# A feed-forward stage whose transposes move from TensorE to VectorE's 32 by 32 squares and an exchange through DRAM

## The chip, the cores and the metric

One core of a Trainium2 chip runs the whole program. The metric is the device time of one execution in microseconds (us), the median of several runs. The engines are named as in the profile: PE (TensorE, with PEld for its weight loads), DVE (VectorE), ACT (ScalarE), POOL (GpSimd) and SP, whose queue issues nearly all DMAs. They run side by side and wait for each other through semaphores. SBUF is the on-chip memory of 128 partitions, PSUM the memory into which PE writes.

## What is computed

Three blocks, each added to x (16 x 64 rows of 512): a cross-attention from x to a context of 16 x 512 rows, a differential self-attention, and a feed-forward block. The change is in the last one alone:

```python
def fp4_quant_dequant(x):                  # blocks of 16 along the last dim
    scale = maximum(max(abs(xb)) / 6.0, 1e-12)
    q = _GRID[searchsorted(_MID, abs(xb / scale))] * sign(xb) * scale
def fp4_linear(x, w):
    return einsum('bsk,nk->bsn', fp4_quant_dequant(x), fp4_quant_dequant(w))
...
xn = layernorm(x)                          # 1024 rows of 512
gate, y = fp4_linear(xn, w_gate), fp4_linear(xn, w_up)      # 1408 columns
h = silu(gate) * y
x = x + fp4_linear(h, w_down)              # back to 512 columns
```

## The kernel before, in words

**Tiles.** The 1024 rows of x are eight row tiles t = 0 to 7 of 128 rows. The 1408 hidden columns are three chunks c = 0, 1, 2 of 512, 512 and 384. A step of the feed-forward stage is one pair (t, c); there are 24, in the order (0,0), (0,1), (1,0), (1,1), (0,2), (1,2), and then (2,0), (2,1), (2,2), (3,0) and so on to (7,2). Steps 0 to 2 are written out by hand among the last pieces of the self-attention (`SelfAttention.rest`, L1623 to L1652). `FeedForward.rest` does the others.

**A step.** `gate` (L1736) and `up` (L1746) multiply the normalised, quantised and transposed x tile by two weight chunks. Each product is three terms: every operand is held as a high and a low half (x as `fx`), and PE adds high x high, high x low, low x high, 12 matmuls for 512 rows of contraction. Both results lie in one PSUM pair `gu`, of which there are two. `gated` (L1753) is ACT's Silu (L1759) and DVE's product (L1760), giving h. `fp4_steps` (L180) quantises h, in order: DVE's block maximum (L194), two small scalings (L195, L196), a reciprocal (L197), the scaling of h by it (L199), the exponent mask (L202), ACT's L205, DVE's L207 and L208, and the scaling back (L210). For h all are on DVE apart from L205; for x, L199 and L210 are on GpSimd. `turn_h` (L1767) transposes h in 128 x 128 squares on PE (`ht`, L171), and `split` (L127) makes the high half `hh` on ACT (L129) and the low half `hl` on DVE (L130). `down` (L1785) multiplies these by w_down and collects `dn` in PSUM over the three chunks of a tile: 12 matmuls, or 9 for chunk 2, of which the last third reads `hl`. After chunk 2 DVE adds x (L1812, `y`) and SP stores the tile.

**The x tiles.** `norm_steps` (L1707) cuts the norm and quantisation of tile t into seven pieces: the moments (DVE, then three small operations on GpSimd, L148 to L160), the shift (ACT, L166), and the five parts of `fp4_steps`. `turn` (L1722) transposes the result on PE (`xt`) and splits it into `fx`.

**Order.** `step(n)` of L1835 names the work of a round: gate of step n, `turn_h` of step n-2, up and `hidden` of n, perhaps a norm, `down` of step n-3, perhaps `turn` of the next x tile. `Common.in_order` (L82) ties every instruction given so far to the one before it on its engine. It is called once, at the end of `SelfAttention.rest` (L1652), so up to there each engine keeps the order of the program (`FeedForward.rest` comes after the call); a scheduler places what comes later, and may put it ahead, between instructions that are tied to each other. Buffers come from pools by tag; a tag with `bufs=1` is one buffer, whose next user waits for the last reader of the one before.

**The chip's own squares.** While the weights are quantised (`Quantise.piece`, L277), DVE transposes each 32 x 32 square of a tile in place of the whole (`nc.vector.transpose`, L287); the weights were rearranged beforehand so that this is enough.

Of the kernel before, what the change touches and what calls it, by code (L numbers as in the profile page):

```python
# [9 lines left out]
F32 = mybir.dt.float32  # L10
F32R = mybir.dt.float32r
# [3 lines left out]
ALU = mybir.AluOpType  # L15
# [4 lines left out]
P = 128  # L20
D = 512
KC = D // P
# [4 lines left out]
NT = B * S // P  # L27
# [18 lines left out]
def f32(t):  # L46

    return t.bitcast(F32)


class Common:
# [125 lines left out]
        for _ in self.fp4_steps(*args, **kwargs):  # L177
            pass

    def fp4_steps(self, pool, w, n, name, first=None, second=None, tag="q_e"):  # L180
        nc = self.nc
        first, second = ((nc.vector, nc.gpsimd)[bool(by)] for by in (first, second))
        nb = n // BLK

        def blocks(t):
            return t.rearrange("p (n b) -> p n b", b=BLK)

        def spread(t):
            return t.unsqueeze(2).to_broadcast([P, nb, BLK])

        m = self.small.tile([P, nb], F32, tag="q_m", name=f"qm_{name}")
        s = self.small.tile([P, nb], F32, tag="q_s", name=f"qs_{name}")
        e = pool.tile([P, n], F32, tag=tag, name=f"qe_{name}")
        nc.vector.tensor_reduce(m, blocks(w), AX.X, ALU.max, apply_absolute_value=True)  # L194
        nc.vector.tensor_scalar(s, m, 1.0 / 6.0, 1e-12, ALU.mult, ALU.max)  # L195
        nc.vector.tensor_scalar(m, s, 1.0 + SHADE, None, ALU.mult)  # L196
        nc.vector.reciprocal(m, m)  # L197
        yield True
        first.tensor_tensor(blocks(w), blocks(w), spread(m), ALU.mult)  # L199
        yield True  # L200

        nc.vector.tensor_scalar(  # L202
            e.bitcast(U32), w.bitcast(U32), 0x7F800000, None, ALU.bitwise_and
        )
        nc.scalar.activation(e, e, AF.Relu, bias=self.mmagic, scale=MAGIC)  # L205
        yield True
        nc.vector.scalar_tensor_tensor(w, e, MAGIC, w, ALU.add, ALU.add)  # L207
        nc.vector.scalar_tensor_tensor(w, w, MAGIC, e, ALU.subtract, ALU.subtract)  # L208
        yield True
        second.tensor_tensor(blocks(w), blocks(w), spread(s), ALU.mult)  # L210
        yield True
# [6 lines left out]
class Scratch:  # L218


    def __init__(self, ctx, tc):
        pool = ctx.enter_context(tc.tile_pool(name="scratch", bufs=1, space=DRAM))

        def dram(name, shape):
            return pool.tile(shape, F32, tag=name, name=name)


        self.q = [dram(f"q_d{g}", [P, KC, GT * P]) for g in range(NT // GT)]
        self.k = [dram(f"k_d{g}", [P, KC, GT * P]) for g in range(NT // GT)]
        self.v = [dram(f"v_d{p}", [P, D]) for p in range(NT)]  # L230
        self.rs = [dram(f"rs_d{b}", [1, N]) for b in range(B)]

        self.gu = {
            (w, c): dram(f"{w}_d{c}", [P, 2, KC, n])
            for w in ("g", "u")
            for c, (_, n) in enumerate(CHUNKS)
        }
        self.dn = [dram(f"d_d{c}", [P, 2, n // P, D]) for c, (_, n) in enumerate(CHUNKS)]


class Quantise:
# [1063 lines left out]
class SelfAttention:  # L1305
# [269 lines left out]
    def rest(self, ff, last):  # L1575

        first, second = (ff.norm_steps(t) for t in range(2))  # L1580
        norms = iter(first[:2] + second[:1] + first[2:4] + second[1:2] + first[4:] + second[2:])


        parts = {3: (1, 0, 1), 4: (1, 2, 1), 5: (1, 2, 0), 6: (0, 2, 0), 7: (1, 2, 0)}

        def steps(n, part):
            for _ in range(parts[n][part] if n in parts else 0):
                next(norms)()

        for n in range(2, NT):  # L1590
            self.product(n, "Wq")
            self.cosines(n, "Wq")
            self.scale(n - 2)
            self.sum(n - 1)
            self.product(n, "Wk")
            if n == NT - 1:
                ff.weights(("g", 1))
            self.mix(n - 1)
            self.turn_o(n - 2)
            self.low_o(n - 2)  # L1600
            self.sines(n, "Wq")
            self.add(n, "Wq")
            self.product(n, "Wv")
            if n == NT - 1:
                ff.weights(("u", 1), ("d", 0))
            self.values(n)
            if n + 1 < NT:
                self.norm(n + 1)
            self.cosines(n, "Wk")
            self.sines(n, "Wk")  # L1610
            steps(n, 0)
            self.add(n, "Wk", self.nc.vector)
            if n == NT - 1:
                ff.turn(0)
            self.out(n - 2)
            last.get(n, lambda: None)()
            if n == 2:
                ff.weights(("g", 0), ("u", 0))
            steps(n, 1)
            self.end(n)  # L1620
            steps(n, 2)
        assert not list(norms)
        self.scale(NT - 2)  # L1623
        self.sum(NT - 1)
        ff.gate((0, 0))
        self.mix(NT - 1)
        ff.up((0, 0))
        ff.gated((0, 0))
        self.turn_o(NT - 2)
        self.low_o(NT - 2)  # L1630
        ff.turn(1)
        ff.gate((0, 1))
        self.turn_w(NT - 1)
        ff.quantise((0, 0))
        ff.weights(("d", 1))
        ff.gate((1, 0))
        self.weigh(NT - 1)
        self.squares(NT - 1)
        self.rms(NT - 1)
        self.out(NT - 2)  # L1640
        ff.weights(("g", 2))
        ff.up((0, 1))
        self.scale(NT - 1)
        ff.hidden((0, 1))
        ff.up((1, 0))
        self.turn_o(NT - 1)
        self.low_o(NT - 1)
        ff.hidden((1, 0))
        ff.turn_h((0, 0))
        self.out(NT - 1)  # L1650
        ff.weights(("u", 2), ("d", 2))
        self.cm.in_order()  # L1652


class FeedForward:


    def __init__(self, tc, cm, sc, w1, w2, out):
        self.tc, self.cm, self.nc, self.sc, self.out = tc, cm, tc.nc, sc, out
        self.w1, self.w2 = w1, w2  # L1660
        self.W, self.st = {}, {}

        self.steps = [(t, c) for t in range(2) for c in range(2)] + [(t, 2) for t in range(2)]
        self.steps += [(t, c) for t in range(2, NT) for c in range(len(CHUNKS))]

    def weights(self, *names):

# [39 lines left out]
    def norm_steps(self, t):  # L1707

        cm, w2, st = self.cm, self.w2, self.st

        def begin():
            st["mv", t] = mv = cm.small.tile([P, 3], F32, tag="mv3", name=f"mv_f_{t}")
            cm.shift(cm.x[t], f"f_{t}", mv)

        def norm():
            z = st["z", t] = w2.tile([P, D], F32, tag=("g_o", "b_o")[t % 2], name=f"fz_{t}")
            cm.shifted(z, cm.x[t], st.pop(("mv", t)))
            st["fp4", t] = cm.fp4_steps(w2, z, D, f"x_{t}", True, True, tag="one")

        return [begin, norm] + 5 * [lambda: next(st["fp4", t])]  # L1720

    def turn(self, t):  # L1722
        cm, w2 = self.cm, self.w2
# [43 lines left out]
    def turn_h(self, s):  # L1767
        cm, w2 = self.cm, self.w2
        t, c = s
        n = CHUNKS[c][1]  # L1770
        nk = n // P
        pt = cm.tr(f"ht_{t}_{c}")
        cm.transpose_chunks(pt, self.st.pop(("h", s)), nk)
        hh = w2.tile([P, KC, P], F32R, tag="two_h", bufs=2, name=f"hh_{t}_{c}")[:, :nk, :]
        hl = w2.tile([P, KC, P], F32R, tag="two_l", bufs=2, name=f"hl_{t}_{c}")[:, :nk, :]
        src = pt[:, :n].rearrange("p (k n) -> p k n", n=P)
        if s == self.steps[-1]:
            for k in range(nk):
                cm.nc.scalar.copy(hh[:, k, :], src[:, k, :])
            cm.nc.vector.tensor_tensor(hl, src, f32(hh), ALU.subtract)  # L1780
        else:
            cm.split(hh, hl, src)
        self.st["hT", s] = hh, hl

    def down(self, s):  # L1785
        cm, nc = self.cm, self.nc
# [45 lines left out]
                nc.vector.tensor_tensor(y[h], both[h], self.cm.x[t][:, cols], ALU.add)  # L1832
                nc.sync.dma_start(self.out[t * P : (t + 1) * P, cols], y[h])

    def step(self, n):  # L1835
        s = self.steps[n] if n < len(self.steps) else None
        if s:
            self.gate(s)
        if 0 <= n - 2 < len(self.steps):
            self.turn_h(self.steps[n - 2])  # L1840
        if s:
            self.up(s)
            self.hidden(s)
            if s[1] == 2 and 2 <= s[0] < NT - 2:
                self.norm(s[0] + 2)
            elif s in ((1, 1), (0, 2)):
                self.norm(1 + s[1])
        if 0 <= n - 3:
            self.down(self.steps[n - 3])
        if s and (s == (1, 2) or (s[1] == 1 and 2 <= s[0] < NT - 1)):  # L1850
            self.turn(s[0] + 1)

    def rest(self):
        for n in range(3, len(self.steps) + 3):
            self.step(n)


@with_exitstack
# [96 lines left out]
```

## Time and profile before

| what | us |
|---|---|
| median of 3 runs (lowest, highest) | 880.55 (878.98, 880.85) |
| the profiled execution's own time | 881.33 |
| its span, first to last instruction | 879.5 |
| PE's matmuls busy | 871.7 |
| DVE busy | 687.2 |
| ACT busy | 398.8 |
| POOL busy | 296.2 |
| share of the chain that ended last: PE | 93% |
| stretch 704 to 879.5: PE, DVE, ACT, POOL busy | 171.54, 143.57, 48.69, 15.53 |

The chain of waits goes back from the last instruction, at each step to what released it; PE has 93% of it. The last row is the feed-forward stage without its first pieces. In the text, a time such as "at 694.87" is counted from the start of the span. Lines of the profile name an engine, the line of the program (that of a helper, if a helper gave the instruction), what is written and read, and the shapes.

### The profile page before, as it was taken

What the parts mean: (1) busy time and instruction counts of PE and PEld (TensorE: products, weight loads), DVE (VectorE), ACT (ScalarE), POOL (GpSimd) and SP (SyncE); (2) the same over time, 40 slices, a digit from 0 to 9 for tenths busy, and PEclk for the clock granted to TensorE, in tenths of its full rate; (3) what the DMA queues carried; (4) which work ended last, traced back from release to release, by engine and by line L of the source; (5) the groups of instructions that cost most, each with busy time, mean ns of one, the idle gap of its engine ahead of it and who ended that gap; (6) DMA issues with size and microseconds to landing.
All of it is one profiled execution on the core that took longest, in us unless ns stands there. A gap on an engine that the chain in (4) does not pass through costs nothing.

```text
span 879.5 us, 17521 instructions
## 1 busy us (share of the span) xinstructions
PE 871.7 (99%) x6743; PEld 719.2 (82%) x6743; DVE 687.2 (78%) x1457; ACT 398.8 (45%) x787; POOL 296.2 (34%) x341
## 2 busy tenths in 40 slices
PE   8999999999999999999999999999999999999998
PEld 8988787878787888778878888888888888888887
DVE  7734457789788887787888867688998897888876
ACT  5654454544544535354445455554556233332221
POOL 2334234235353352353433622545543120111100
PEclk9999999999999999999999999999999999999999
DMA  8464554644655455435644362240008330000000
GB/s 277 167 233 169 167 163 142 201 143 141 192 164 160 138 174 168 136 111 178 183 134 149 121 198 64 82 192 1 1 3 320 136 144 13 13 13 13 13 12 25
DMA packets 80379, 111.12 MB, mean 126 GB/s; under 512 B 33176, under 2 KB 39080, under 8 KB 79016
## 3 DMA queue, kind: packets, MB, share of 16 engines
q1 hardware_dynamic: 80136, 109.48, 38.2%
q8 instruction: 53, 0.87, 0.4%
q0 software_dynamic: 160, 0.52, 0.2%
q14 instruction: 30, 0.25, 0.1%
HBM read 84.26 MB, written 25.72 MB: 125 GB/s over the span
## 4 chain that ended last, share of the span: by engine, by line
PE 93%; DVE 3%; DMA 2%; ACT 1%; POOL 1%; issue 1%; SPq 0%; ACTq 0%; DVEq 0%; POOLq 0%
PE pv L121 20%; PE pk L121 19%; PE gu L121 13%; PE dn L121 6%; PE sim L967 4%; PE av L1055 4%; PE Wv L121 3%; PE wo L121 3%; PE po L121 2%; PE Wq L121 2%; PE Wk L121 2%; PE prt L1004 2%; PE lq L121 2%; PE lk L121 2%; PE lv L121 1%; PE ht L171 1%
## 5 line engine op out<-in xcount | busy, mean ns | idle before, releaser
L121 PE MATMUL pv<-xvh,x 128*128 128x512 f32 x512 | 133.0, 394 | 0.0
L121 PE MATMUL pk<-x,xkh 128*128 128x512 f32 x512 | 128.2, 392 | 0.0
L121 PEld LDWEIGHTS pv<-xvh,x 128*128 128x128 f32 x512 | 94.8, 188 | 26.2 <-issue 7.0
L121 PEld LDWEIGHTS pk<-x,xkh 128*128 128x128 f32 x512 | 94.9, 188 | 19.5 <-issue 0.4
L990 ACT ACTIVATE pr<-pr,least 128x576 f32<-128x576 f32 x64 | 49.1, 769 | 59.7 <-DVE least L986 59.7
L941 DVE TENSOR_TENSOR k<-pk,row 128x512 f32<-128x512 f32 x64 | 43.2, 675 | 39.2 <-PE pk L121 39.0
L368 POOL TENSOR_TENSOR x<-raw,x 128x512 fp32r<-128x512 f32 x32 | 41.6, 1301 | 85.8 <-ACT x L362 80.5
L121 PE MATMUL pv<-xvl,x 128*128 128x512 f32 x256 | 68.7, 390 | 0.0
L121 PE MATMUL pk<-x,xkl 128*128 128x512 f32 x256 | 68.5, 389 | 0.0
L954 ACT ACTIVATE v<-pv,rs 128x512 f32<-128x512 f32 x64 | 43.2, 684 | 54.8 <-PE pv L121 54.3
L121 PE MATMUL gu<-uT,fx 128*128 128x512 f32 (+1 forms) x288 | 67.0, 377 | 0.2 <-DMA uT<-u_d 0.2
L121 PE MATMUL gu<-gT,fx 128*128 128x512 f32 (+1 forms) x288 | 65.8, 376 | 0.0
L121 PEld LDWEIGHTS gu<-gT,fx 128*128 128x128 f32 x288 | 52.2, 188 | 7.6 <-ACT fx L129 0.2
L121 PEld LDWEIGHTS gu<-uT,fx 128*128 128x128 f32 x288 | 51.8, 188 | 7.7 <-DMA uT<-u_d 0.5
L121 PEld LDWEIGHTS pv<-xvl,x 128*128 128x128 f32 x256 | 48.0, 188 | 10.3
L121 PEld LDWEIGHTS pk<-x,xkl 128*128 128x128 f32 x256 | 48.1, 188 | 10.2
L986 DVE CUSTOM_DVE_ANT_0 pr<-sim,mask 128x576 f32<-128x576 f32 x64 | 45.8, 753 | 5.3 <-PE sim L967 4.3
L205 ACT ACTIVATE qe_h<-qe_h,mmagic 128x512 f32<-128x512 f32 (+1 forms) x24 | 16.5, 687 | 66.7 <-DVE qe_h L202 64.6
L321 DVE BATCH_NORM_STATS2 cst<-nat 128x6 f32<-128x512 f32 x64 | 42.8, 669 | 3.7 <-DMA nat<-in_ctx_dram 3.7
L121 PE MATMUL dn<-dT,hh 128*128 128x512 f32 x170 | 42.9, 392 | 0.0
L967 PE MATMUL sim<-k,mask 64*64 64x288 f32 x512 | 40.4, 415 | 0.3 <-DMA mask<-q_d 0.3
L362 ACT CAST x<-raw 128x512 fp32r<-128x512 f32 x64 | 39.1, 631 | 0.0
(347 smaller groups left out, 1867.1 us busy)
## 6 DMA issues: line engine op xcount, KB each, us to landing
nat<-in_ctx_dram SPq DMA_DIRECT2D x16, 1024.0 KB
raw<-in_ctxT_dram SPq DMA_DIRECT2D x64, 256.0 KB
d_d<-qhl_d SPq DMA_DIRECT2D x11, 512.0 KB
row<-rs_d SPq DMA_DIRECT2D x16, 256.0 KB
g_d<-qhl_g SPq DMA_DIRECT2D x8, 512.0 KB
u_d<-qhl_u SPq DMA_DIRECT2D x8, 512.0 KB
gT<-g_d SPq DMA_DIRECT2D x4, 1024.0 KB
uT<-u_d SPq DMA_DIRECT2D x4, 1024.0 KB
```

The costliest lines, as they stand in the source:

```text
L121: self.nc.tensor.matmul(ps, lhsT=p[i], rhs=p[j], start=start and n == 0, stop=stop and n == last)
L205: nc.scalar.activation(e, e, AF.Relu, bias=self.mmagic, scale=MAGIC)
L321: nc.vector.bn_stats(st, self.nat[b][:, j, :])
L362: self.cm.nc.scalar.copy(self.done[b][0][:, c, :], self.raw[:, c, :])
L368: by.tensor_tensor(lo, self.raw[:, c, :], f32(hi), ALU.subtract)
L941: nc.vector.tensor_tensor(k[:, S : S + N], ps, cx.row[b], ALU.mult)
L954: nc.scalar.mul(v, ps, cx.rs[b][:, t : t + 1])
L967: nc.tensor.matmul(pss[r][c * S : (c + 1) * S, h, :half], lhsT=queries[b % 2][rows, m, :], rhs=st["k"][m][rows, at : at + half], start=Tru ...
L986: nc.vector.tensor_tensor_reduce(two(pr), ps[:, :, :half], two(mask), -1.0, BIG, ALU.add, ALU.min, least)
L990: nc.scalar.activation(pr, pr, AF.Exp, bias=least, scale=-1.0, accum_out=st["tot"][:, t : t + 1])
L1004: nc.tensor.transpose(pt[:, c, at : at + S], state[b]["pr", a][rows, r, first + j * P : first + (j + 1) * P], cm.ident[rows, rows],)
L1055: nc.tensor.matmul(st["av"][r][rows, a, :], lhsT=prT[:, j, rows], rhs=st["v"][j][:, at : at + S], start=False, stop=j == NJ - 1, skip_grou ...
```

## The change

The transposes of the x tiles 3 to 7, and of h in the 19 steps from (1,1) to (7,0) (`far_steps`), leave PE. In their place DVE transposes 32 x 32 squares (`squares`, after the change L1728), SP writes the result to a DRAM scratch in four DMAs, one for each 32 partitions (L1735), and reads it back in the order of a full transpose with a fifth (L1737). `halves` then makes the high half on ACT (L1744) and the low half on GpSimd (L1745) from SBUF. For the same 19 steps the scaling back of h, L210, goes to GpSimd. `turn_h` of step n-2, the halves included, now stands at the end of round n, after the whole quantisation of h of step n, and the squares of step n-1 stand in round n between L202 and L207. The x tiles' pieces are put by `begin_x` at fixed places of the rounds: part 0 between L205 and L207 of h, part 1 after h. For t >= 2 the x quantisation's scratch shares the tag "tri" with h. `in_order` is called after `FeedForward.rest`, so the whole program keeps its written order on every engine.

```diff
-    def fp4_steps(self, pool, w, n, name, first=None, second=None, tag="q_e"):
+    def fp4_steps(self, pool, w, n, name, first=None, second=None, tag="q_e", bufs=1):
...
-        e = pool.tile([P, n], F32, tag=tag, name=f"qe_{name}")
+        e = pool.tile([P, max(n, D)], F32, tag=tag, bufs=bufs, name=f"qe_{name}")[:, :n]
...
+        self.sq = [dram(f"sq_d{n}", [4, 32, 4, KC * 32]) for n in range(4)]
...
         ff.weights(("u", 2), ("d", 2))
-        self.cm.in_order()
...
+        self.far, self.far_steps = 0, self.steps[3:-2]
...
-            st["fp4", t] = cm.fp4_steps(w2, z, D, f"x_{t}", True, True, tag="one")
+            tag, bufs = ("tri", 3) if t >= 2 else ("one", 1)
+            st["fp4", t] = cm.fp4_steps(w2, z, D, f"x_{t}", True, True, tag=tag, bufs=bufs)
...
+    def squares(self, src, nk, pool, tag, home, name):
+        nc = self.nc
+        t = self.w1.tile([P, 4, KC * 32], F32, tag=tag, name=f"sq_{name}")[:, :, : nk * 32]
+        nc.vector.transpose(
+            t.rearrange("p q (k l) -> p q k l", l=32),
+            src.rearrange("p (k q l) -> p q k l", q=4, l=32),
+        )
+        far = self.sc.sq[self.far % len(self.sc.sq)][:, :, :, : nk * 32]
+        self.far += 1
+        for n in range(4):
+            nc.sync.dma_start(far[:, :, n].rearrange("q f r -> f q r"), t[n * 32 : (n + 1) * 32])
+        raw = pool.tile([P, 4, KC * 32], F32, tag=home, name=f"sr_{name}")[:, :, : nk * 32]
+        nc.sync.dma_start(raw, far.rearrange("q f t r -> (q f) t r"))
+        return raw
+
+    def halves(self, hi, lo, raw):
+        src = raw.rearrange("p t (k l) -> p k t l", l=32)
+        hi, lo = (x.rearrange("p k (t l) -> p k t l", l=32) for x in (hi, lo))
+        self.nc.scalar.copy(hi, src)
+        self.nc.gpsimd.tensor_tensor(lo, src, f32(hi), ALU.subtract)
+
+    def send(self, t):
+        self.st["zs", t] = self.squares(self.st.pop(("z", t)), KC, self.w2, "k1", "four0", f"x_{t}")
+
+    def send_h(self, n):
+        s = self.steps[n]
+        if s in self.far_steps:
+            pool, home = ((self.w1, "k2"), (self.w2, "sq"))[n % 2]
+            nk = CHUNKS[s[1]][1] // P
+            self.st["hs", s] = self.squares(self.st.pop(("h", s)), nk, pool, "k0", home, f"h_{s[0]}_{s[1]}")
+
+    def regroup(self, t):
+        both = self.w2.tile([P, 2, KC, P], F32R, tag=f"fx{t % 2}", name=f"fx_{t}")
+        self.halves(both[:, 0], both[:, 1], self.st.pop(("zs", t)))
+        self.st["x", t] = both[:, 0], both[:, 1]
...
     def turn_h(self, s):
...
+        if s in self.far_steps:
+            self.halves(hh, hl, self.st.pop(("hs", s)))
+            return
...
+    def begin_x(self):
+        at = {n: ([], []) for n in range(len(self.steps))}
+        for t in range(2, NT):
+            x = self.norm_steps(t)
+            send, half = (lambda t=t: self.send(t)), (lambda t=t: self.regroup(t))
+            if t == 2:
+                plan = ((3, 0, x[:2]), (3, 1, x[2:4]), (4, 0, x[4:5]), (4, 1, x[5:]))
+                plan += ((5, 1, [lambda t=t: self.turn(t)]),)
+            elif t == 3:
+                plan = ((4, 1, x[:2]), (5, 0, x[2:4]), (5, 1, x[4:5]), (6, 0, x[5:]))
+                plan += ((6, 1, [send]), (7, 1, [half]))
+            else:
+                n = 3 * t - 8
+                plan = ((n, 0, x[:1]), (n + 1, 0, x[1:2]), (n + 2, 0, x[2:4]), (n + 3, 0, x[4:5]))
+                plan += ((n + 4, 0, x[5:]), (n + 5, 0, [send]), (n + 6, 1, [half]))
+            for n, part, jobs in plan:
+                at[n][part].extend(jobs)
+        return at
+
-    def step(self, n):
+    def step(self, n, at):
         s = self.steps[n] if n < len(self.steps) else None
         if s:
             self.gate(s)
-        if 0 <= n - 2 < len(self.steps):
+            self.up(s)
+            self.gated(s)
+            h = self.cm.fp4_steps(
+                self.w2, self.st["h", s], CHUNKS[s[1]][1], f"h_{s[0]}_{s[1]}", False, s in self.far_steps, tag="one"
+            )
+            for _ in range(3):
+                next(h)
+            self.send_h(n - 1)
+            for job in at[n][0]:
+                job()
+            for _ in h:
+                pass
+            for job in at[n][1]:
+                job()
             self.turn_h(self.steps[n - 2])
-        if s:
-            self.up(s)
-            self.hidden(s)
-            if s[1] == 2 and 2 <= s[0] < NT - 2:
-                self.norm(s[0] + 2)
-            elif s in ((1, 1), (0, 2)):
-                self.norm(1 + s[1])
-        if 0 <= n - 3:
-            self.down(self.steps[n - 3])
-        if s and (s == (1, 2) or (s[1] == 1 and 2 <= s[0] < NT - 1)):
-            self.turn(s[0] + 1)
+        self.down(self.steps[n - 3])
+        if not s and n - 2 < len(self.steps):
+            self.turn_h(self.steps[n - 2])
 
     def rest(self):
+        at = self.begin_x()
         for n in range(3, len(self.steps) + 3):
-            self.step(n)
+            self.step(n, at)
+        self.cm.in_order()
```

More of the change, by code (lines that the diff above doesn't have):

```diff
@@ L1771, in turn_h @@
         nk = n // P
+        hh = w2.tile([P, KC, P], F32R, tag="two_h", bufs=2, name=f"hh_{t}_{c}")[:, :nk, :]
+        hl = w2.tile([P, KC, P], F32R, tag="two_l", bufs=2, name=f"hl_{t}_{c}")[:, :nk, :]
+        self.st["hT", s] = hh, hl
+        if s in self.far_steps:
+            self.halves(hh, hl, self.st.pop(("hs", s)))
+            return
         pt = cm.tr(f"ht_{t}_{c}")
         cm.transpose_chunks(pt, self.st.pop(("h", s)), nk)
-        hh = w2.tile([P, KC, P], F32R, tag="two_h", bufs=2, name=f"hh_{t}_{c}")[:, :nk, :]
-        hl = w2.tile([P, KC, P], F32R, tag="two_l", bufs=2, name=f"hl_{t}_{c}")[:, :nk, :]
         src = pt[:, :n].rearrange("p (k n) -> p k n", n=P)
@@ L1782, in turn_h @@
             cm.split(hh, hl, src)
-        self.st["hT", s] = hh, hl
     def down(self, s):
```

## The prediction

> **What bounds the kernel now.** I read the page's busy shares first, then the feed-forward stage in stretches of one row tile, then the chain of waits there.
>
> ```profile
> PE 871.7 (99%) x6743; PEld 719.2 (82%) x6743; DVE 687.2 (78%) x1457; ACT 398.8 (45%) x787; POOL 296.2 (34%) x341
> ```
>
> ```profile
> 792.30:816.60 24.30, 24.30 (x122) 20.85 (x120) 20.94 (x42) 6.58 (x11) 2.21 (x2) 1.00 0.03 11
> 816.60:840.90 24.30, 24.30 (x121) 20.84 (x121) 20.93 (x43) 6.56 (x11) 2.22 (x2) 1.00 0.03 11
> ```
>
> The columns are the stretch, then busy time of PE, PEld, DVE, ACT and POOL, PE's clock, DMA share. One tile takes 24.3 us, PE is never idle and at full clock, DVE works 20.9 us, GpSimd 2.2. So here a microsecond off PE is a microsecond off the end, as long as nobody else is late. The chain of waits prices PE's work:
>
> ```profile
> 714.49 0.44 PE ht L171 x4
> ...
> 719.00 4.57 PE dn L121 x20
> 723.57 0.44 PE xt L171 x4
> ...
> 736.59 2.07 PE dn L121 x9
> ```
>
> A transpose costs 0.11 us, a 512-column matmul 0.2285 (4.57 over 20); 384 columns come to 0.1735 (2.08 over 12, at 788 and 790). I call U the moment at which PE leaves a step's up product. After U come dn(n-3), then gate and up of step n+1.
>
> **What goes.** 19 of 24 h tiles lose their PE transposes (12 x 4 + 7 x 3 = 69) and five x tiles theirs (20): 89 x 0.11 = **-9.8 us**. DVE loses 19 scalings (L210, 0.69, 0.55 at 384), 19 hl and 5 fx subtractions, and gains 24 transposes; per tile 20.9 - 1.9 - 1.9 - 0.7 + 2.6 + 0.9 (moments, which the scheduler had put into the attention) = 19.9 us. GpSimd's 2.2 us per tile become 2.2 + 3.0 (h's scalings) + 4.9 (four low halves) + 1.2 (moments) = 11.3. Neither sum exceeds PE's 24.3 - 1.7 = 22.6. What matters is the order.
>
> **Prices not in the trace.** The new square transpose: nearest is L287, 0.69 us; ends 0.42 (L202) and 1.23 (L1469); I take 0.69. The low half on GpSimd from a strided source: nearest is L368 (1.30), ends 1.06 (L210) and 1.59 (L1472, strided); I take 1.30, 1.0 at 384.
>
> ```profile
> L368 POOL TENSOR_TENSOR x<-raw,x 128x512 fp32r<-128x512 f32 x32 | 41.6, 1301 | 85.8 <-ACT x L362 80.5 <-DMA k<-k_d 5.3
> L210 POOL TENSOR_TENSOR fz<-fz,qs_x 128x512 f32<-128x512 f32 x8 | 8.9, 1112 | 44.8 <-DVE fz L208 21.2 <-DVE qm_h L196 19.3 <-DVE qm_x L196 4.3
> ```
>
> The exchange: four writes at 0.33 to 0.61 us of issue, 1.2 us from the last issue to landing (row rs_d), then a read, 2.0 us from issue to landing (out_dram at 739.78): 4.6 to 6 us. An h tile is sent about U + 5 and wanted some 9 us later, an x tile has about 4 us to spare; I cost it at nothing. On SP's queue only the y stores stand behind it, and nobody waits for them within a tile. If a hop took 2 us more, h would still be covered, and five x tiles would lose at most 1 us each.
>
> **The chain of one step**, from the timeline at 785 to 791 and 800: Silu starts U + 0.20, DVE's h product U + 0.83, then block maximum +0.73, the three small operations +0.72, +0.21, +0.22, scaling +0.38, exponent mask (L202) +0.73, so U + 3.82; through ACT's L205 to L207 +1.27 or more, L208 +0.72, done 0.69 later; GpSimd starts 0.15 after that. In the new program DVE does the previous tile's squares and x's pieces between L202 and L207, and GpSimd does h's scaling (1.1), x's low half if it is due, and only then the low half of the tile two steps back. PE wants that one in the next step, at the ninth of twelve dn matmuls (seventh of nine).
>
> - Chunk 0 of a tile, with x's squares and block maximum between: L208 ends U + 8.24, scaling to 9.5, low half to 10.85. PE is there at 3 x 2.74 + 1.82 = U + 10.0: a **stall of 0.9**.
> - Chunk 1, with x's mask and moments between: L208 ends U + 7.56, GpSimd's three small moments operations end about U + 7.6, scaling 8.8, x's low half 10.15, low half at 384 11.2. PE is there at 2.74 + 2 x 2.08 + 1.37 = U + 8.3, or 9.2 after the stall before: 2.1. DVE's L195 and L196 of the next steps then meet GpSimd's operations. The next lines show such meetings: L202 at 384 columns takes 1.09 instead of 0.35, L199 1.24 instead of 0.69, with a GpSimd operation alongside:
>
> ```profile
> 796.62 1.09 DVE L202 TENSOR_SCALAR qe_h<-h 128x384 uint32<-128x384 uint32 x1
> ...
> 804.35 1.24 DVE L199 TENSOR_TENSOR h<-h,qm_h 128x512 f32<-128x512 f32 x1
> ```
>
> That adds about 0.5: a **stall of 2.6**.
> - Chunk 2: low half at U + 8.4 to 9, wanted at U + 9.4 and later: none.
>
> L207 and L208 average 0.69 like L210 without company, so I let them run beside GpSimd. The Trainium skill, "SBUF — State Buffer", section "Who interferes with whom", says that a VectorE instruction with two inputs in SBUF also waits for a GpSimd instruction that reads SBUF; by that rule x's first scaling, which now lies beside L207 and L208 of chunk 0, would cost up to 1.1 us in each of three tiles, 3.3 us more; no row here shows these two lines blocked in general.
>
> **The sum, in order of time.**
>
> 1. The last wo product. Before, PE goes from ht straight into gu of (1,1) at 694.87 and takes wo later; in program order wo comes first and waits for oh:
>
> ```profile
> 694.87 2.98 PE L121 MATMUL gu<-gT,fx 128*128 128x512 f32 x12
> ...
> 697.26 0.62 ACT L1539 CAST oh<-oT 128x512 fp32r<-128x512 f32 x1
> ```
>
> 697.95 - 694.87 = **+3.1**. wo ends sooner, so the u weights that wait for its slots come sooner: their 7.2 us of DMA are covered.
> 2. Steps (0,2) to (2,0). DVE in order does h(0,2), x2's and x4's pieces, x3's moments; ACT's hh(1,0) stands behind x3's shift, which waits for those moments on GpSimd. With U at 713.5 of the old clock, DVE's h product is at 715.65 and its L208 of x2 ends at 722.95; x2's scaling ends 724.15, so xt(2) starts there though PE was free at 720.85 (3.35); moments, shift and hh end at 726.85, so dn(1,0) waits 2.2; it ends at 729.6. Silu of (1,2) was behind hh as well, so L202 of (1,2) is at 730.1, and after ACT's L205 and x4's shift fx(2) is at 732.6: 3.05. **+8.6**.
> 3. dn(0,2) and dn(1,2): low halves at 749.4 and 758.3, wanted at 747.7 and 755.65: **+4.3**.
> 4. The pair of stalls above behind tiles 3 and 4, 2 x 3.5 = **+7.0**; at tile 5, without moments, 0.9 + 1.6 = **+2.5**; at tile 6, without x's mask, **+1.8**.
> 5. The tail. hh(7,0) stands on ACT behind L205 of (7,2), at U + 4.3 to 4.9, while PE ends dn(6,2) at U + 2.1; and ht(7,1) follows dn(7,0) in place of preceding it. dn_last starts at U + 12.7, and 5.8 us follow (873.72 to 879.5); before, U at 864.80, all took 14.7. 18.5 - 14.7, and 0.4 because a transpose in it is already counted: **+4.2**.
>
> Sum: 3.1 + 8.6 + 4.3 + 7.0 + 2.5 + 1.8 + 4.2 - 9.8 = +21.7. The profiled execution took 881.33 (span 879.5 and 1.8 around it), so 903.0; it lies 0.8 above the median of 880.55, so **902** against the runs shown.
>
> The trace has no idle stretch of PE over 0.41 us in this stage, and its clock is 1.00 in all stretches. "TensorE: Matmul & The Clock Gate" of the Trainium skill, section "Part 1: The HAM clock gate", says that an idle window of about 3.4 us halves the clock until a busy one has passed; that would make the 3.35 us gap cost up to 1.7 us more, and no run here shows it.
>
> **Rivals.**
>
> - **Only the ends stall** (17%). If far steps keep up, because GpSimd's operations take the low ends or DVE meets fewer of them, terms 3 and 4 go: 902 - 15.6 = 886. For it: neither engine is full. Against it: 11.2 us against 8.3.
> - **Loads decide, not chains** (12%): the other side. If low halves reach PE within 8.3 us of U at 384 columns and 10.0 at 512, and x2 is ready when PE is, PE stays the bound and only wo's wait and the saving are left: 880.55 - 9.8 + 3.1 = 874. The point is the chunk 1 chain: it has to lose 2.9 us of 11.2.
> - **GpSimd and the exchange dearer** (14%): low halves at 1.59 and squares at 1.23 lengthen about ten binding chains by 0.5 to 0.8 each: 902 + 8 = 910.
> - **It does not take hold** (2%): the saving and the stalls are both small, 880.
>
> **How the numbers follow.** The forecast, 902 with about 6 either way, has 55%. To hold 8 in 10 the range takes in the second case and most of the dear one: 885 to 910. Faster by over 0.2% (about what a measurement of this kernel can tell from no change) has 0.12, within 0.02, slower 0.86.
>
> **What would show it.** PE idle in the feed-forward stage of some 31 us with GpSimd (hl) and ACT (hh, fx, oh) as releasers; a tile from 24.3 us to about 26 in the middle; PE's ht and xt groups down to 19 and 12 instructions in the whole program; DVE not over 21 us per tile. If PE idles under 10 us, chains are shorter than I have them; if squares' DMAs release ACT or GpSimd, the exchange was not hidden.

## The result, and the profile after

| | us |
|---|---|
| before, median (lowest to highest) | 880.38 (878.98 to 880.85) |
| after, median (lowest to highest) | 906.54 (904.82 to 907.86) |
| ratio, 95% interval | 1.0299, 1.0274 to 1.0323 |
| after's profiled execution, its span | 907.86, 906.1 |

The kernel is 3.0% slower: 26.2 us, where 21.7 were forecast. First the busy shares of the kernel after:

```profile
PE 873.2 (96%) x6654; PEld 715.2 (79%) x6654; DVE 692.3 (76%) x1438; ACT 398.0 (44%) x787; POOL 348.0 (38%) x384
```

PE has 6743 - 6654 = 89 instructions less, as counted, but it is busy 1.5 us longer, and its idle time in the span went from 7.8 to 32.9. So the 26.6 us between the two spans are 25.1 of idle time, less 9.8 for the transposes, and 11.3 by which the remaining work takes longer than it did. The idle time by releaser, in the waits of PE from 690 on (total us, times, longest):

```profile
PE dn L121 <- POOL hl L1745: 13.1, 9, 2.3
PE dn L121 <- ACT hh L1744: 3.5, 3, 2.9
PE dn L121 <- ACT hh L129: 3.3, 3, 1.9
PE xt L171 <- POOL fz L210: 3.0, 1, 3.0
PE wo L121 <- ACT oh L1540: 2.7, 1, 2.7
PE dn_last L1867 <- ACT hh L1823: 0.4, 1, 0.4
```

The first line is the low half on GpSimd, in nine places; the others are the casts and the x tile at both ends of the stage. Most of the other 11.3 us is the clock. These stretches of the kernel after show it (length, busy time of PE, PEld, DVE, ACT, POOL, then PE's clock):

```profile
725.00:731.80 6.80, 6.02 (x14) 4.33 (x15) 5.69 (x15) 2.91 (x6) 0.52 (x1) 0.50 0.08 21
759.00:762.40 3.40, 3.40 (x10) 2.62 (x9) 3.30 (x7) 1.83 (x3) 0.93 (x1) 0.51 0.24 58
786.40:789.80 3.40, 3.40 (x9) 2.67 (x8) 3.28 (x7) 1.83 (x3) 0.43 (x1) 0.50 0.12 29
888.80:895.60 6.80, 5.96 (x16) 4.67 (x16) 3.37 (x4) 0.79 (x2) 1.27 (x1) 0.50 0.10 39
```

Half clock for 20.4 us in all, each time shortly after one or two gaps of 1.9 to 3.0 us. dn(1,0) and dn(7,0) take 5.49 instead of 2.74, three gate products 0.7 to 1.6 more: 9 of the 11.3 us. The rest I did not place.

One tile, the counterpart of the two stretches of before:

```profile
787.28:814.76 27.48, 24.29 (x106) 20.09 (x105) 22.17 (x41) 7.12 (x12) 12.07 (x12) 0.95 0.29 82
```

27.5 us instead of 24.3, and VectorE is busy 22.2 us where 19.9 of work were reckoned. The timeline in that tile says why. The number behind the start is the duration; a bracket at the end holds the idle time before it:

```profile
800.70 1.38 POOL L199 TENSOR_TENSOR fz<-fz,qm_x 128x512 f32<-128x512 f32 x1 [7.43 <-DVE qm_x L197]
...
801.20 1.43 DVE L208 SCALAR_TENSOR_TENSOR h<-h,qe_h 128x512 f32<-128x512 f32 x1
...
803.80 1.26 POOL L1745 TENSOR_TENSOR hl<-sr_h,hh 128x512 fp32r<-128x512 f32 x1
...
804.34 0.76 DVE L195 TENSOR_SCALAR qs_h<-qm_h 128x32 f32<-128x32 f32 x1
...
805.12 1.19 PE L121 MATMUL dn<-dT,hl 128*128 128x512 f32 x4 [1.08 <-POOL hl L1745]
```

GpSimd's L199 ends at 802.08, and L208 (0.69 alone) at 802.63, about as if it had begun only then; L195 (0.18 alone) ends at 805.10, right behind the low half at 805.06. PE starts at the same moment. Between 745 and 865 L208 averages 0.99 at 512 columns and 1.30 at 384:

```profile
L208 DVE SCALAR_TENSOR_TENSOR h<-h,qe_h 128x512 f32<-128x512 f32 x10 | 9.9, 986 | 0.3
L208 DVE SCALAR_TENSOR_TENSOR h<-h,qe_h 128x384 f32<-128x384 f32 x4 | 5.2, 1299 | 0.1
```

The mean at 512 columns hides two cases: 1.43 beside x's scaling L199, 0.69 elsewhere; at 384 columns it is x's L210 that lies beside it. Both are operations that GpSimd had before. What moved to GpSimd meets other lines: the low half L1745 holds up L195 and L196, 0.72 to 0.92 instead of 0.18 at three places of this tile.

The new operations, from the groups of the kernel after (count, busy us, mean ns):

```profile
L1745 POOL TENSOR_TENSOR hl<-sr_h,hh 128x512 fp32r<-128x512 f32 x12 | 15.3, 1279 | 7.1 <-ACT hh L1744 5.4 <-DMA sr_h<-sq_d 1.7
L1728 DVE STREAM_TRANSPOSE sq_h<-h 128x512 f32<-128x512 f32 x12 | 8.5, 704 | 0.0
L1745 POOL TENSOR_TENSOR hl<-sr_h,hh 128x384 fp32r<-128x384 f32 x7 | 7.1, 1010 | 4.8 <-ACT hh L1744 4.8
```

1.28, 0.70 and 1.01 stand against 1.30, 0.69 and 1.0 in the prediction.

### The profile page after: what moved, and what is told of

Read it like the earlier page. It is cut to its first block, busy times and chain, and to the rows that moved or that the text cites. A ratio compares the mean times of both kernels' runs of the same rounds, so it can differ in the third digit from the quotient of the medians.

```text
span 906.1 us, 17584 instructions
## 1 busy us (share of the span) xinstructions
PE 873.2 (96%) x6654; PEld 715.2 (79%) x6654; DVE 692.3 (76%) x1438; ACT 398.0 (44%) x787; POOL 348.0 (38%) x384
## 4 chain that ended last, share of the span: by engine, by line
PE 83%; DVE 8%; POOL 4%; issue 2%; ACT 1%; DMA 1%; SPq 1%; DVEq 0%; POOLq 0%; ACTq 0%
PE pv L121 20%; PE pk L121 19%; PE gu L121 9%; PE sim L968 4%; PE av L1056 4%; PE dn L121 3%; PE wo L121 2%; PE Wv L121 2%; PE lv L121 2%; PE po L121 2%; PE Wq L121 2%; PE Wk L121 2%; PE prt L1005 2%; PE lq L121 2%; PE lk L121 2%
## 5 line engine op out<-in xcount | busy, mean ns | idle before, releaser
L121 PE MATMUL gu<-gT,fx 128*128 128x512 f32 (+1 forms) x288 | 68.0, 386 | 0.0
L121 PE MATMUL gu<-uT,fx 128*128 128x512 f32 (+1 forms) x288 | 63.9, 371 | 0.0
L121 PEld LDWEIGHTS gu<-gT,fx 128*128 128x128 f32 x288 | 55.0, 196 | 10.0 <-ACT fx L129 0.6
L205 ACT ACTIVATE qe_h<-qe_h,mmagic 128x512 f32<-128x512 f32 (+1 forms) x24 | 16.5, 689 | 90.0 <-DVE qe_h L202 90.0
L121 PE MATMUL dn<-dT,hh 128*128 128x512 f32 x170 | 46.6, 418 | 6.8 <-ACT hh L1744 3.5
L121 PEld LDWEIGHTS dn<-dT,hh 128*128 128x128 f32 x170 | 33.4, 201 | 15.3 <-ACT hh L1744 4.6
```

The costliest lines, as they stand in the source:

```text
L121: self.nc.tensor.matmul(ps, lhsT=p[i], rhs=p[j], start=start and n == 0, stop=stop and n == last)
```

## The experiments

The theory at the start: the places that the written order gives to a few operations make PE wait, and the waits halve its clock. Against it: the exchange's latency, GpSimd's load and its meetings with VectorE, or the order as such. Ratios are against the kernel before, on the same chip.

**1. The order without the squares.**

```diff
-        self.far, self.far_steps = 0, self.steps[3:-2]
+        self.far, self.far_steps = 0, []
...
-            send, half = (lambda t=t: self.send(t)), (lambda t=t: self.regroup(t))
+            send, half = (lambda: None), (lambda t=t: self.turn(t))
```

> The written order for the whole program is kept, but all transposes stay on PE (no squares, no exchange, h's scaling and all low halves on VectorE). Theory (the loss lies in where the order puts the low half and the few casts): the same chains without GpSimd in them. By the rows of the kernel after, the low half of a 512-column tile is then done about U + 9.6 and PE wants it at U + 10.4, that of a 384-column tile at 8.8 against 8.7, so the middle hardly stalls; wo's 2.7, the early steps' 3 to 5 and about 2 at the end stay, with 2 to 4 more for the halved clock: 886 to 894. Rival A (the order by itself is the loss, whatever engine does the work): 900 or more, with hl on VectorE as PE's releaser in the middle. Rival B (GpSimd and the exchange are the whole loss, the order costs nothing): 880 to 883.

Measured: 900.77, ratio 1.0223 (1.0205 to 1.0242). PE's longest waits:

```profile
PE dn L121 <- ACT hh L129: 3.7, 3, 2.2
PE wo L121 <- ACT oh L1540: 2.7, 1, 2.7
PE xt L171 <- POOL fz L210: 2.5, 1, 2.5
PE ht L171 <- DVE hl L130: 2.0, 1, 2.0
PE dn L121 <- DVE hl L130: 1.4, 1, 1.4
```

The theory has the place right (between 755 and 881 PE waits in one spot, 0.24 us), the number wrong: I had 6 to 14 us for the two ends of the stage, and it is 20. That is the size of rival A, though hl in the middle isn't the releaser. Three quarters of the loss are there without a single square; the squares, in this order, add 6 where they take 9.8 off PE. L208 is as long here as in the kernel after, though h's scaling and all low halves are back on VectorE: it is the order that puts it beside x's scalings.

```profile
L208 DVE SCALAR_TENSOR_TENSOR h<-h,qe_h 128x512 f32<-128x512 f32 x10 | 9.9, 985 | 0.3
```

**2. The squares without the order.** `in_order` goes back to the end of the attention's `rest`.

```diff
         ff.weights(("u", 2), ("d", 2))
+        self.cm.in_order()
...
             self.step(n, at)
-        self.cm.in_order()
```

> Squares, exchange and h's scaling on GpSimd as in the kernel after, but the order of the feed-forward is left to the scheduler (the written order ends with the attention, as before). Theory: the work itself fits beside PE, so without the fixed places most of the 26 us of PE's idle time and the 9 us of half clock go: 873 to 886. Rival (GpSimd, its meetings with VectorE and the exchange are too dear in any order): 898 or more, with PE still waiting for hl from GpSimd over 10 us.

Measured: 887.18, ratio 1.0075 (1.0058 to 1.0091), one microsecond above my range. The clock stays near 1.00 (0.996) and wo no longer waits; what is left is mostly this:

```profile
PE dn L121 <- ACT hh L1745: 10.2, 8, 3.7
PE xt L171 <- POOL fz L210: 1.3, 1, 1.3
```

hh waits for the read here: ACT waits 34.8 us in 14 places for h's reads, never in the kernel after, and the chain that ended last has 7% of DMA in it, where after has 1%. The scheduler's order is better than the written one by 19 us, but it makes the exchange late.

**3. The halves earlier in the step.** `turn_h` moves up, nothing else changes.

```diff
             self.send_h(n - 1)
+            self.turn_h(self.steps[n - 2])
...
                 job()
-            self.turn_h(self.steps[n - 2])
```

> One place is moved: the halves of the tile two steps back are issued right behind the previous tile's squares, ahead of x's pieces and of h's scaling, instead of at the end of the step. Every instruction stays. Theory: the low half is then done about U + 6.5 and wanted at U + 8.3 at the earliest, so PE's 13.1 us behind hl and the 1.9 behind hh of (1,0) go, and the half clock at 759 and 786 (3.2 us) with them; wo, xt and the end stay: 906.5 - 13.1 - 1.9 - 3.2 = 888, between 885 and 892. Rival A (the exchange's latency is what the low half waits for): GpSimd or ACT then wait for the read, PE's idle time stays above 20 us, 900 to 907. Rival B (VectorE and GpSimd meeting each other set the pace of a tile): 897 to 906 with PE waiting in gu for h's or fx's later halves.

Measured: 902.14, ratio 1.0242 (1.0227 to 1.0257). The first fence is PE's longest waits, the second the tile:

```profile
PE dn L121 <- ACT hh L1744: 7.1, 5, 3.2
PE xt L171 <- POOL fz L210: 6.6, 1, 6.6
PE gu L121 <- POOL fx L1745: 3.7, 3, 1.3
PE gu L121 <- ACT fx L129: 2.9, 1, 2.9
```

```profile
787.26:812.63 25.37, 23.18 (x105) 19.26 (x105) 24.48 (x41) 6.92 (x12) 12.71 (x12) 1.00 0.33 89
```

hl is gone from the list, all 13.1 us, and a third of them is won. VectorE is now busy 24.5 of 25.4 us: GpSimd's low halves fell upon L207 and L208 (at 384 columns they average 1.43 and 1.37 instead of 0.55). Other halves then come late. Of rival A only the time fits: ACT waits 4.2 us for x's reads and never for h's. In the middle this is rival B, and my theory falls in its simple form: it is not enough to move the operation that PE waits for, it matters what VectorE does beside it. But part of the loss lies elsewhere. From the up product of (2,0) to dn(6,2) the profile is 9.4 us shorter than the kernel after's; ahead of that, from the up product of (1,2) on, it is 3.6 longer. There VectorE's low halves of (0,1) and (1,0), each after a wait for hh (1.32 and 0.60), now stand before x2's moments and mask, so xt(2) waits 6.6 us instead of 3.0. That is the place in the order again, and no meeting with GpSimd.

**4. No exchange.** The halves read the squares tile itself, which takes the buffer of the read.

```diff
-        t = self.w1.tile([P, 4, KC * 32], F32, tag=tag, name=f"sq_{name}")[:, :, : nk * 32]
+        t = pool.tile([P, 4, KC * 32], F32, tag=home, name=f"sq_{name}")[:, :, : nk * 32]
...
-        far = self.sc.sq[self.far % len(self.sc.sq)][:, :, :, : nk * 32]
...
-        nc.sync.dma_start(raw, far.rearrange("q f t r -> (q f) t r"))
-        return raw
+        return t
```

> The exchange through DRAM is left out: the halves read the squares as VectorE wrote them, so the columns of the outputs are not the reference's; every instruction on the engines and their order stay. Theory: the exchange is hidden but for 1 to 2.5 us (ACT's wait for x's read at tiles 5 to 7, 2.4 us in the trace, in front of hl): 903.5 to 906.5. Rival A (the exchange's latency stands in the chain of hl): the mid stalls go, 895 or less.

Measured: 906.05, ratio 1.0288 (1.0267 to 1.0309), and 12.9 us of waits for hl. The exchange through DRAM costs nothing that can be measured in this order.

**5. PE kept busy in its gaps.** 82 matmuls (the expectation's 70 was miscounted; they are 12 + 8 + 9 + 7 + 4 + 8 + 4 + 8 + 4 + 2 + 1 + 2 + 11 + 2).

```diff
+    def busy(self, n, at):
+        for _ in range(self.fill.get((n, at), 0)):
+            self.nc.tensor.matmul(
+                self.pair(n + 1)[:, 0, :],
+                lhsT=self.W["g", 0, 0][0][:, :P],
+                rhs=self.W["g", 0, 0][0],
+                start=True,
+                stop=True,
+            )
...
```

> The kernel after, with matmuls of no use put where PE waits (70 of 512 columns, each 0.23 us at full clock, into the PSUM pair that the next gate product overwrites): 12 before xt(2), 8 before dn(1,0), 9 and 7 before the low halves of dn(0,2) and dn(1,2), 4 and 8 or fewer for those of the tiles, 11 before dn(7,0). No wait is taken away. Theory (idle time halves PE's clock afterwards, 20.5 us in all at 0.5, which costs about 9): the granted clock stays at 1.00 to the end, and the time falls by 4 to 8, the rest coming back as longer waits for the same releasers: 899 to 903. Rival (the slow stretches only fill time that PE would have waited anyway): 905 to 909 with the clock at 1.00.

Measured: 908.11, ratio 1.0309 (1.0288 to 1.033). The page's clock row is at 9 in all 40 slices, and the time did not fall. In the profile, the stretch from the gate of (1,1) to dn_last is 198.1 us against 201.5, and 2.8 of the 3.4 are dn(7,0) at full clock; the middle gains 0.6. The same execution lost 3.1 ahead of that stretch, half of it because wo's own gap, which I had not filled, halved the clock there, the other half before any gap. And with dn(1,0) at full clock a wait comes up that the kernel after hid behind it:

```profile
734.31 4.41 PE L121 MATMUL gu<-gT,fx 128*128 128x512 f32 x12 [2.39 <-ACT fx L129]
```

In the kernel after, the gate of (2,0) waits 0.6 at most. So my reading of the profile after, 9 us lost to the clock, falls: where another engine's chain is due later anyway, the slow matmuls lie in time that PE would have waited. Only where PE itself is the chain, at dn(7,0), do they cost what they look like.

**6. h's last scaling back on VectorE.**

```diff
-                self.w2, self.st["h", s], CHUNKS[s[1]][1], f"h_{s[0]}_{s[1]}", False, s in self.far_steps, tag="one"
+                self.w2, self.st["h", s], CHUNKS[s[1]][1], f"h_{s[0]}_{s[1]}", False, False, tag="one"
```

> h's last scaling goes back to VectorE; squares, exchange, low halves on GpSimd and the order stay. Theory 1 (the low half is late because it stands behind the scaling on GpSimd): the low half runs as soon as hh is cast, the 13 us behind hl go with the half clock in the middle, nothing new comes: 888 to 892. Theory 2, which the run with the halves first speaks for (VectorE and its meetings with GpSimd set a tile's pace): hl's wait goes too, but VectorE gains 1.9 us of scaling in a tile and loses about 1 of meetings, tiles take 24.5 to 26 and PE waits for h, hh or fx in place of hl: 895 to 902.

Measured: 909.78, ratio 1.0323 (1.0306 to 1.034). PE's two largest waits, then a tile:

```profile
PE dn L121 <- ACT hh L1744: 11.8, 6, 2.9
PE dn L121 <- POOL hl L1745: 3.9, 4, 1.8
```

```profile
790.08:816.25 26.17, 23.24 (x106) 19.20 (x105) 24.84 (x44) 7.02 (x12) 10.01 (x9) 1.00 0.31 86
```

GpSimd has 2 us less in a tile, VectorE 2.7 more and is full; hh takes hl's place. Beside a low half on GpSimd VectorE's L210 takes 1.67 at 512 columns and 1.53 at 384. Theory 1 is out. Theory 2 has the cause, though I priced it 8 us too low. In this order, moving the scaling to GpSimd is thus no loss by itself: it neither makes nor cures the stalls.

**7. wo after the gate of (1,1).**

```diff
...
+        ff.gate((1, 1))
         self.out(NT - 1)
...
```

The step of (1,1) then begins with its up product.

> One place is moved: the gate product of (1,1) is issued ahead of the last wo product, as the scheduler had it before. Theory: PE works on it while oh is made, the wait of 2.7 us is gone and nothing behind it is late: 903 to 904.5. Rival (the next wait takes it over, hh of (1,0) or xt(2), whose releasers don't depend on PE): 905.5 to 907.

Measured: 905.42, ratio 1.0276 (1.0254 to 1.0297). wo's 2.7 us are gone, and the next wait takes them: dn(0,1) waits 2.49 for hh instead of 0.67. The two ratios overlap, so a gain over the kernel after isn't shown; the rival is nearer.

**8. A new order, every instruction kept.** x2's and x3's moments earlier, squares behind the block maximum, halves right behind h's product, x's block maximum and moments behind L208, ht(7,1) before dn(7,0), wo as in 7. The main part of the edit:

```diff
...
             self.gated(s)
+            for job in at[n][2]:
+                job()
+            self.turn_h(self.steps[n - 2])
...
-            for _ in range(3):
-                next(h)
+            next(h)
             self.send_h(n - 1)
+            for _ in range(2):
+                next(h)
...
-                plan = ((n, 0, x[:1]), (n + 1, 0, x[1:2]), (n + 2, 0, x[2:4]), (n + 3, 0, x[4:5]))
-                plan += ((n + 4, 0, x[5:]), (n + 5, 0, [send]), (n + 6, 1, [half]))
+                plan = ((n, 1, x[:1]), (n + 1, 0, x[1:2]), (n + 2, 1, x[2:4]), (n + 3, 0, x[4:5]))
+                plan += ((n + 4, 0, x[5:6]), (n + 4, 1, x[6:]), (n + 5, 0, [send]), (n + 7, 2, [half]))
...
```

> A written order meant to cure all of it, with every instruction of the kernel after: gate of (1,1) before wo; x2's and x3's moments and shifts in the attention's last step; the previous tile's squares behind the block maximum, the halves of x and of the tile two steps back right behind VectorE's h product (so that GpSimd's low halves fall beside block maximum and scaling and not beside L207 and L208); x's block maximum and moments behind L208; ht(7,1) before dn(7,0). Theory (places, not work, are the loss; VectorE without meetings needs 20.2 us of work and 1.2 between instructions in a tile): tiles of 22.7 to 24, full clock, 873 to 882. Rival (VectorE is full in any order): tiles of 25 or more, 885 to 900.

Measured: 886.0, ratio 1.0053 (1.0036 to 1.007). 20 us of the 26 are back, though not the forecast 873 to 882: the time lies at the edge of the rival's range, the tile in the theory's. PE's longest waits and a tile:

```profile
PE dn L121 <- ACT hh L129: 4.6, 1, 4.6
PE gu L121 <- POOL fx L1747: 3.9, 3, 1.5
PE dn L121 <- ACT hh L1746: 1.1, 1, 1.1
```

```profile
780.65:804.48 23.83, 22.88 (x105) 19.32 (x105) 22.29 (x42) 6.98 (x13) 11.03 (x12) 1.00 0.35 95
```

The tile is shorter than before's 24.3. The first line is of my making: the Silu of (1,0) now stood behind the shifts of x2 and x3.

**9. The second new order**, which takes these three lines on. Against the kernel of 8, in its main part; h(7,0) goes back to PE, so 18 h tiles keep their squares:

```diff
-        self.far, self.far_steps = 0, self.steps[3:-2]
+        self.far, self.far_steps = 0, self.steps[3:-3]
...
-        ff.hidden((0, 1))
+        ff.hidden((0, 1), 2)
...
+        self.early[x] = self.norm_steps(x)
+        self.early[x][0]()
...
-                plan += ((n + 4, 0, x[5:6]), (n + 4, 1, x[6:]), (n + 5, 0, [send]), (n + 7, 2, [half]))
+                plan += ((n + 4, 0, x[5:6]), (n + 4, 1, x[6:]), (n + 5, 0, [send]), (n + 6, 1, [half]))
...
```

> The new order, with its remaining waits of PE (11.6 us) taken on one by one: x2's and x3's moments into VectorE's gaps ahead of L207 of (0,1) and (1,0), their shifts behind hh(0,0), so that Silu of (1,0) no longer stands behind them (4.65 at dn(0,0)); x's halves ahead of x's moments at the end of the step before (fx 4.7 in three tiles); x2's pieces half a step earlier (0.7); h(7,0) turned on PE (hh 1.07, price 0.44). Theory (waits of PE that are taken away come off the end as long as VectorE has room, 20.2 + 1.2 of 22.65 us in a tile): 886.0 - 8 to 10 = 876 to 878, so faster than before by about 0.4%. Rival (VectorE and its meetings with GpSimd already set the pace, the waits move): 881 to 886.

> The same kernel once more, a second look at the same order for the spread of the profile: within 1.5 of the run beside it.

Measured: 877.69, ratio 0.997 (0.9957 to 0.9982): faster than before by 0.3%, and as forecast. A single further execution took 878.12. A tile:

```profile
772.65:795.93 23.28, 22.89 (x105) 19.31 (x105) 21.74 (x41) 7.13 (x12) 11.27 (x12) 1.00 0.34 93
```

L207 and L208 are at 0.69 each again. The meetings went to L202 (0.36 to 1.00 at 384 columns; before had 0.95 there) and L196 (0.18 to 0.49), and VectorE has less than 1.6 us of the tile left. PE waits 6.0 us in all; that a still better order would give these back isn't shown.

**10. The second order without squares.** The edit of 1 in the kernel of 9.

> The second new order with all transposes on PE again: no squares, no exchange, h's scaling and all low halves on VectorE. Theory (once the order is right the squares are worth PE's time that they save, 84 transposes of 0.11 or 9.2 us, less the 5.9 us of waits that fx's and hl's late halves leave): PE has 9.2 us more work, VectorE fits (about 23 of 24.3 us in a tile), and the time is 877.7 + 3 to 6 = 881 to 884. Rival A (the order alone gives the gain over before, the squares nothing): 876 to 879. Rival B (with VectorE doing its own scalings and low halves this order stalls): 888 or more.

Measured: 881.52, ratio 1.0014 (1.0005 to 1.0023). PE waits 1.7 us in all. So in a good order the squares, the exchange and the scaling on GpSimd are worth 0.44%, 3.9 us of the 9.4 that they take off PE (6743 - 6658 = 85 transposes, where the expectation has 84); the order alone is worth nothing over before, rival A is out. Set beside experiment 1, it is the same work on the same engines with the same buffers in another order: 900.77 there, 881.52 here.

**11. The second order with the x tiles turned on PE.** Only the line with `send, half` of 1.

> The second new order with the x tiles turned on PE (four transposes and VectorE's low half in place of squares, exchange and GpSimd's low half, for tiles 3 to 7); the h tiles keep squares and exchange. Theory (the waits that are left, 3.6 us for fx's halves in tiles 3 to 6, come from x's late exchange and GpSimd): they go for 5 x 0.44 = 2.2 us of PE, 876 to 877.5. Rival (xt's own halves are as late, since ACT and VectorE take them in the same place): 878.5 to 881.

Measured: 877.83, ratio 0.9973 (0.9962 to 0.9983): the same as 9, between theory and rival. The 2.1 us of waits for fx's low half on GpSimd are gone, 20 transposes of 0.11 cost 2.2 us, and two waits for fx on ACT stay (1.4, in 9 1.5).

## Why the prediction was right, and where it was not

The side and the mechanism were right: PE no longer sets the pace alone, and it waits for GpSimd's hl in the middle and for casts at both ends. Step by step:

1. wo: 3.1 forecast, 2.7 measured. Experiment 7 shows that it was not all on the path: the next wait takes most of it. I had priced the wait, not asked who is late behind it.
2. Steps (0,2) to (2,0), 8.6: xt(2) 3.03 (forecast 3.35), dn(1,0) 1.93 (2.2), the gate of (2,0) 0.6 instead of 3.05. Experiment 5 shows that third wait at 2.39 when PE keeps its clock; in the kernel after, dn(1,0) at half clock lies in its place.
3. dn(0,2) and dn(1,2): 4.3 forecast, 2.34 + 1.90 = 4.24 measured.
4. Tiles 3 and 4: 0.9 and 2.6 forecast for each pair, 1.07 and 2.11, 1.08 and 2.11 measured; tile 5 2.5 against 1.8, tile 6 1.8 against 1.2. The reasons were right in kind: hl stands on GpSimd behind h's scaling and x's low half. But the chain that I summed is only one round of a loop (Silu, VectorE, GpSimd, dn, next Silu), and experiment 3 shows that cutting it at hl gives back 4 us of 13: VectorE is the next limit of a tile, and at the start of the stage x2 comes 3.6 later.
5. The tail: 4.2 forecast. From U of (7,2), 884.5, to the end of the span, 906.1, it takes 21.6 instead of 14.7: hh(7,0) comes 2.87 late, and dn(7,0) then runs at half clock, 2.75 more. This clock is what was missing; experiment 5 gives it back there (dn(7,0) to dn_last 8.0 us instead of 10.7).

Two steps failed.

"L207 and L208 average 0.69 like L210 without company, so I let them run beside GpSimd." L208 did not: 0.99 and 1.30 in the middle. Nor did L207 in experiment 3, where GpSimd's low half is already running when it begins (1.43 at 384 columns). The Trainium skill, "SBUF — State Buffer", section "Who interferes with whom", says that a VectorE instruction with two inputs in SBUF contends with a GpSimd instruction that reads SBUF; here the measurement is on its side. My row was no evidence, since GpSimd had only 2.2 us of work per tile before and hardly ever lay beside these lines. In the tile at 787.28 that is 0.74 for L208 at 512 columns and 0.75 at 384; L195 and L196 beside the low halves add 1.9, where I had about 0.5. So VectorE came to 22.2 us in a tile where I had written "not over 21". In the kernel after that is still 5 us less than the tile takes: VectorE is late at single places there, and not full.

The clock, "up to 1.7 us". It was halved for 20.4 us. The Trainium skill, "TensorE: Matmul & The Clock Gate", "Part 1: The HAM clock gate", asks for an idle window of about 3.4 us; here gaps of 1.9, 2.1 and 2.9 us were enough (before 758.17, 786.07 and 889.64), while another of 2.1 us (before 813.97) did nothing, and wo's 2.7 us halved the clock in experiment 5 and not in the kernel after. The stretches of 3.4 and 6.8 us agree with its window, once and twice. What it cost is less than it looks: 2.8 us at the end are shown, more is not.

That the exchange costs nothing was right for this order (experiment 4); in the scheduler's it makes hh late (experiment 2). And the two errors lie on opposite sides of the sum: idle time grew by 25.1 in place of 31.5, and PE's remaining work by 11.3, 9 of it at half clock, in place of nothing. That the total came out within 5 us is in part luck: the one stands in the place of the other.

## What to carry to other kernels

When work moves from an engine that is full to one that is free, ask what the free one holds up: here VectorE instructions took up to 1.15 us longer beside an operation of GpSimd (L196 in experiment 9), and the order decides which of them it meets. A wait that is named in a profile is worth its time only if nothing else is due just behind it: taking away 13 us of hl gave 4, taking away wo gave 1 at most, and keeping the clock up in the gaps gave nothing. The same instructions took 906 or 886 us by their order alone, and 878 with one h tile back on PE, so try a new split of work in a good order before judging it.

## What the runs showed of the hardware

- The halved clock outlasts the gap by far: the gap from 886.8 to 889.6 is followed by half clock up to 895.6, though PE is busy in all but 0.8 us of the last 6.8.
- VectorE's small operations stand still like the long ones: L196, on 128 x 24 elements, takes 0.18 us alone and 0.97 on average in the middle of experiment 3, as L195 takes 0.76 at 804.34 above. The squares (0.70) and the block maximum (0.69) keep their time in all runs, with GpSimd beside them.
- GpSimd is held up too when it starts second. L207 at 800.54 keeps its time (0.63), and L199, which GpSimd begins beside it at 800.70, takes 1.38 instead of 1.06. GpSimd's moments step L149, on a single column, takes 1.00 at 809.35, beside L208, and 0.55 at 723.50, where VectorE is idle; it averages 0.82 in the kernel after against 0.61 before.
